# A convolution's rows gathered by head before normalising and transposing, instead of taken in their natural tiles

## The chip, the cores and the metric

The kernel runs on one core of one Trainium2 chip. The metric is the device time of one execution in microseconds (us). A profiled execution gives the trace; its span runs from the first to the last instruction. Engines are TensorE (PE, with PEld for its weight loads), VectorE (DVE), ScalarE (ACT), GpSimd (POOL) and SyncE (SP), which here only issues transfers.

## The reference, cut to what matters

Two layers, each a gated cross attention and a gated feed-forward, on x of shape (8, 256, 512). The change lies in the first layer's "attention", which is a long convolution:

```python
    def _L0_xattn_ref(k, v, q, ssm_kernel, D, head_dim):
        ...
        H = HD // head_dim
        fft_size = 2 * L
        ...
        kv = jnp.einsum('bhil,bhjl->bijhl', k_, v_)
        kv_f = jnp.fft.rfft(kv, n=fft_size)
        kernel_f = jnp.fft.rfft(ssm_kernel, n=fft_size)
        y = jnp.fft.irfft(kv_f * kernel_f, n=fft_size)[..., :L]
        out = y + kv * D[None, None, None, :, None]
        out = jnp.einsum('bijhl,bhil->bjhl', out, q_)
        ...
    x = x + jnp.tanh(g_xattn[0]) * _L0_xattn_ref(ctx_2048, ctx_2048, _layernorm(x, axis=-1), L0_xattn_ssm_kernel, L0_xattn_D, 8)
    x = x + jnp.tanh(g_ffn[0]) * _L0_ffn_ref(_layernorm(x, axis=-1), L0_ffn_w1, L0_ffn_w2, L0_ffn_w3)
    x = x + jnp.tanh(g_xattn[1]) * _L1_xattn_ref(_layernorm(x, axis=-1), ctx_2048, mask_BxS2_bk0)
    x = x + jnp.tanh(g_ffn[1]) * _L1_ffn_ref(_layernorm(x, axis=-1), L1_ffn_w1, L1_ffn_w2, L1_ffn_w3)
```

Context and x have 256 rows per batch, k and v are both the context and q is the normalised x. The 256 rows of a batch are 32 heads of 8 rows; the convolution runs along the 512 columns. Each row is normalised over those 512 columns.

## The kernel before

**Tiles.** x is 2048 rows of 512, kept for the whole kernel in `xs` as 16 natural tiles of 128 rows. A natural tile is half a batch: the even tiles hold heads 0 to 15 of the eight batches, the odd ones heads 16 to 31. The convolution wants positions on the partitions, so every tile is normalised (statistics and their aggregate on DVE, L116 and L117; square root on ACT, L121; reciprocal and the negative mean term on DVE, L126 and L134; the norm itself on ACT, L179, or DVE, L174), turned by four PE transposes into one PSUM tile `tr` (L386), and copied by ACT into the buffer `qT` (`keep_x`, L389; in the opening three of these by DVE, L657). Head 0 needs its 8 rows of every batch, and so all eight even tiles.

**One head.** The convolution is a product with a Toeplitz matrix: `load_toep` (L270) fetches its 128 x 512 strip from `ssm_skip`, a copy of the padded kernel in DRAM to which the skip term D has been added, and `load_ch` fetches the context (L265). ACT doubles the context (`ctx_twice`, cx, L289), POOL multiplies its 36 row pairs (`pair_products`, kv, L302 and L308), PE runs 10 matmuls of 288 columns in two halves (`half_matmuls`, L325), which the profile shows as 6 and 14 instructions, because each fp32 matmul stands there as two (a transpose as one), into one of three PSUM tiles `y`, ACT repeats some columns (`half_wrap`, L335), DVE multiplies by q in three instructions per half (`half_products`, L347, L353, L360), POOL adds the two planes (`add_halves`, L370) and DVE reduces them into `qT` (`reduce_terms`, L375). In steps 12, 14, 19 and 21 (the set `alone`), POOL's sum is left out and DVE reduces both planes (L377). q is doubled before it is used, by one ACT copy per head out of `qT` (`q_twice`, L289).

**Order.** The whole stage is written out by hand: each engine executes its instructions in program order, and a wait holds up all that stands behind it on that engine. After the opening a loop runs over 32 steps h; `half_matmuls(h + 1, 1)` and `half_matmuls(h + 2, 0)` belong to step h. A table of jobs adds other work to the slots of a step ("load", "act", "dve", "pe", "act2", "pool", "late"): the odd x tiles in steps 0 to 12, the absolute values, rounding and clipping of the feed-forward weights (`w0`, `w1`), the transposes back with the first residual (L394, L204, steps 17 to 25), and the statistics for the next stage. All these transfers are issued by SP, also in program order. Strips, contexts and kv have three buffers each, the doubled context and q two.

**The opening** normalises the even tiles in four pairs: two 256 KB tiles per transfer (L259), statistics of the second pair placed before the inverse of the first, `half_matmuls(0, 0)` after the first pair's transposes, the rest of head 0 among those of the other three pairs. Five small transfers go out from ACT's queue (gates, the skip term in two layouts, the padded kernel); the first strip comes directly from the input, and its diagonal gets the skip term from DVE (L286). ACT loads the Tanh table for the gates before the Sqrt table.

Of the kernel before, what the change touches and what calls it, by code (L numbers as in the profile page):

```python
# [9 lines left out]
F32 = mybir.dt.float32  # L10
# [32 lines left out]
def flamingo_gated_kernel(  # L43
# [48 lines left out]
    gates_in = small.tile([P, 4], F32, name="gates_in")  # L92
# [132 lines left out]

    s_conv, s_load, s_y = ExitStack(), ExitStack(), ExitStack()
# [14 lines left out]
    ssm = big.tile([H, P + L], F32, name="ssm")  # L241
    skip = big.tile([H, 1], F32, name="skip")
    d0 = big.tile([P, 1], F32, name="d0")

    anti = wl.tile([P, 3 * L], F32, tag="w0st", name="anti")[:, :P]
# [4 lines left out]
    )  # L250
    ssm_skip = dram.tile([H, P + L], F32, name="ssm_skip")
# [5 lines left out]
    def load_x(ts):  # L257
        sl = slice(ts[0], ts[-1] + 1, 2)
        nc.sync.dma_start(out=xs[:, sl, :], in_=x_tiles[:, sl, :])  # L259
# [3 lines left out]
    def load_ch(h):  # L263
        chs[h] = p3.tile([P, NL * B, HD], F32, tag="ch", name="ch")
        nc.sync.dma_start(out=chs[h].rearrange("p a i -> p (a i)"), in_=ctx_heads[h])  # L265
# [11 lines left out]
    def first_toep():  # L277

        toeps[0] = p3.tile([P, L], F32, tag="toep", name="toep")
        nc.sync.dma_start(  # L280
            out=toeps[0], in_=bass.AP(ssm_pad.tensor, ssm_pad.offset + 1, [[1, P], [1, L]])
        )

    def first_diagonal():
        t = toeps[0][:, :P]
        nc.vector.scalar_tensor_tensor(t, anti, d0[:, 0:1], t, op0=ALU.mult, op1=ALU.add)  # L286

    def twice(out, src):
        nc.scalar.copy(  # L289
            out.rearrange("p a (r i) -> p a r i", r=2),  # L290
            src.unsqueeze(2).to_broadcast([P, NL * B, 2, HD]),
        )

    def ctx_twice(h):
        cxs[h] = p2.tile([P, NL * B, HX], F32, tag="cx", name="cx")
        twice(cxs[h], chs[h])
# [15 lines left out]
    def q_twice(h):  # L312
        qxs[h] = p2.tile([P, NL * B, HX], F32, tag="qx", name="qx")
        twice(qxs[h], qT[:, :, h * HD : (h + 1) * HD])
# [22 lines left out]
    def half_products(h, half):  # L337


        if half == 0:  # L340
            prods[h] = p2.tile([P, 2, NL * B, HD, ND], F32, tag="prod", name="prod")
        prod = prods[h]
        n = 2 * B
        yv = ys.pop((h, half)).rearrange("p k b n -> p (k b) n")
        r = slice(half * n, (half + 1) * n)
        q = qxs[h][:, r, :]
        nc.vector.tensor_tensor(  # L347
            prod[:, 0, r, :, :],
            yv[:, :, W0 : W0 + ND * HD].rearrange("p a (i d) -> p a i d", d=ND),
            view(q, [HX, n], [1, HD], [1, ND]),  # L350
            ALU.mult,
        )
        nc.vector.tensor_tensor(  # L353
            prod[:, 1, r, :, 0].rearrange("p a (r i) -> p a r i", r=2),
            yv[:, :, W0 + ND * HD : W0 + NPAIR].unsqueeze(2).to_broadcast([P, n, 2, ND]),
            view(q[:, :, ND:HX], [HX, n], [ND, 2], [1, ND]),
            ALU.mult,
        )

        nc.vector.tensor_tensor(  # L360
            prod[:, 1, r, :, 1:ND],
            view(yv[:, :, ND - 1 : YB], [YB, n], [ND, HD], [ND - 1, NW]),
            view(q[:, :, HD - NW : HX], [HX, n], [1, HD], [1, NW]),
            ALU.mult,
        )
# [16 lines left out]

    def transpose_x(t, xn):
        tr = trs[t] = ps_tr.tile([P, NL, P], F32, tag="tr", name="tr")
        for c in range(NL):
            nc.tensor.transpose(tr[:, c, :], xn[:, c * P : (c + 1) * P], ident)  # L386

    def keep_x(t):
        nc.scalar.copy(rows[:, :, t * P : (t + 1) * P], trs.pop(t))  # L389
# [132 lines left out]
    lno, lnx, firsts = {}, {}, {}  # L522

    def odd_stats(k):
        mv = small.tile([P, 1, 2], F32, tag="mvo", name="mvo")
        ln_moments(mv, 0, odds[k])
        lno[k] = (mv,)

    def odd_sqrt(k):
        lno[k] += (ln_sqrt(lno[k][0], 1, "o"),)  # L530

    def odd_inverse(k):
        mv, std = lno[k]
        rstd = ln_inverse(std, 1, "o")
        lno[k] = (rstd, ln_nmr(nc.vector, mv, rstd, [0], "o"))

    def odd_norm(k):
        xn = lnx[k] = p2.tile([P, L], F32, tag="xn", name="xn")
        ln_apply_act(xn, odds[k], *lno.pop(k), 0)

    def odd_turn(k):
        transpose_x(odds[k], lnx.pop(k))
# [15 lines left out]
    for k in range(len(odds)):  # L558
        job(k, "load", load_x, [odds[k]])
        job(k + 2, "dve", odd_stats, k)  # L560
        job(k + 2, "late", odd_sqrt, k)
        job(k + 3, "dve", odd_inverse, k)
        job(k + 3, "late", odd_norm, k)
        job(k + 4, "pe", odd_turn, k)
        job(k + 5, "act", keep_x, odds[k])
    for k in range(len(evens)):
        job(17 + k, "pe", back_transpose, evens[k])
        job(18 + k, "dve", back_add, evens[k])
# [10 lines left out]
    steps1 = [2, 7, 8, 9, 10, 12, 13, *range(15, 19), 18, 19, 20, 21, 23]  # L579
# [23 lines left out]


    for g, o in ((g_xattn, 0), (g_ffn, 2)):
        nc.scalar.dma_start(out=gates_in[:, o : o + 2], in_=g.partition_broadcast(P))
    nc.scalar.dma_start(out=d0, in_=ssm_d[0:1].partition_broadcast(P))
    nc.scalar.dma_start(out=ssm, in_=ssm_pad)
    nc.scalar.dma_start(out=skip, in_=ssm_d.rearrange("(h o) -> h o", o=1))
    pairs = [evens[k : k + 2] for k in range(0, len(evens), 2)]  # L610
    load_x(pairs[0])
    load_ch(0)
    first_toep()
    for k in range(1, len(pairs)):
        load_x(pairs[k])
    load_ch(1)
    load_table(AF.Tanh)
    nc.scalar.activation(gates, gates_in, AF.Tanh)
    load_table(AF.Sqrt)

    ps_ = {}

    def pair_stats(k, j):
        if j == 0:
            ps_[k] = (small.tile([P, 2, 2], F32, tag="mvp", name="mvp"),)
        ln_moments(ps_[k][0], j, pairs[k][j])

    def pair_sqrt(k):
        ps_[k] += (ln_sqrt(ps_[k][0], 2, "p"),)

    def pair_inverse(k, by_act):

        mv, std = ps_[k]
        rstd = ln_inverse(std, 2, "p")
        nmr = ln_nmr(nc.vector, mv, rstd, by_act, "p")
        both = wl.tile([P, 3 * L], F32, tag="w0st", name="xnp")
        xn = [both[:, :L], both[:, L : 2 * L]]
        for j in range(2):
            if j not in by_act:
                ln_apply(xn[j], pairs[k][j], mv, rstd, j)  # L640
        ps_[k] = (xn, rstd, nmr)

    def pair_norm(k, by_act):
        xn, rstd, nmr = ps_[k]
        for j in by_act:
            ln_apply_act(xn[j], pairs[k][j], rstd, nmr, j)

    def pair_turn(k, js=(0, 1)):
        for j in js:
            transpose_x(pairs[k][j], ps_[k][0][j])  # L650

    def pair_keep(k, j, eng):
        t = pairs[k][j]
        if eng is nc.scalar:
            keep_x(t)
        else:
            nc.vector.tensor_copy(rows[:, :, t * P : (t + 1) * P], trs.pop(t))  # L657

    pair_stats(0, 0)
    pair_stats(0, 1)  # L660
    ctx_twice(0)
    pair_products(0)
    pair_sqrt(0)
    pair_stats(1, 0)
    pair_inverse(0, (0, 1))
    pair_norm(0, (0, 1))
    first_diagonal()
    pair_stats(1, 1)
    pair_turn(0)
    pair_sqrt(1)  # L670
    half_matmuls(0, 0)
    nc.vector.tensor_add(ssm[:, P : P + 1], ssm[:, P : P + 1], skip)
    nc.sync.dma_start(out=ssm_skip, in_=ssm)
    load_toep(1)
    load_ch(2)
    load_toep(2)
    load_ch(3)
    pair_stats(2, 0)
    pair_keep(0, 0, nc.scalar)
    pair_inverse(1, (0,))  # L680
    pair_norm(1, (0,))
    pair_keep(0, 1, nc.scalar)
    pair_stats(2, 1)
    pair_turn(1, (1, 0))
    pair_sqrt(2)
    pair_stats(3, 0)
    half_matmuls(0, 1, (0,))
    pair_keep(1, 1, nc.scalar)
    pair_inverse(2, (0,))
    pair_norm(2, (0,))  # L690
    pair_stats(3, 1)
    pair_turn(2, (1, 0))
    pair_sqrt(3)
    pair_keep(1, 0, nc.scalar)
    pair_inverse(3, (0,))
    pair_norm(3, (0,))
    ctx_twice(1)
    pair_products(1)
    pair_keep(2, 1, nc.vector)
    half_wrap(0, 0)  # L700
    pair_turn(3, (1, 0))
    pair_keep(2, 0, nc.vector)
    pair_keep(3, 1, nc.scalar)
    pair_keep(3, 0, nc.vector)
    half_matmuls(0, 1, (1,))
    q_twice(0)
    half_wrap(0, 1)
    ctx_twice(2)
    pair_products(2)
    half_matmuls(1, 0)  # L710
    half_products(0, 0)
# [3 lines left out]
    for h in range(H):  # L715
# [5 lines left out]
        if h + 1 < H:  # L721
            q_twice(h + 1)
# [4 lines left out]
        if h > 0 and h - 1 not in alone:  # L727
            reduce_terms(h - 1, True)
        if h in alone:
            reduce_terms(h, False)  # L730
        else:
            add_halves(h)
        if h + 1 < H:
# [588 lines left out]
```

## Time and profile before

| | |
|---|---|
| three executions | 767.15, 771.16 and 1251.91 us, median 771.16 |
| the profiled execution | 769.82 us, its span 768.0 us |
| mean granted TensorE clock | 0.993 |
| busy: PE, DVE, ACT, POOL | 728.3, 594.1, 366.5, 254.3 us |
| first convolution matmul | 14.28 us from the span's start |
| last convolution matmul begins | 190.9 us |
| 640 convolution matmul instructions | 164.2 us of PE, 413 ns mean of one |
| 62 wrap copies of 192 columns, ACT | 303 ns each |
| 64 copies of 512 columns (cx and qx), ACT | 619 to 621 ns each |
| statistics of one tile, DVE | 684 and 182 ns |
| transfers of ch, toep and one x tile | 4.1, 3.8 and 4.7 us from issue to landing, medians |

The slices of the profile are fortieths of the span, each digit the busy share in tenths. In a table of stretches, each engine has its busy time and the number of its instructions. In a timeline a line gives start, duration, engine, source line, operation, result and source, and in brackets the idle time of the engine before it with what ended that. Matmuls overlap, so that a matmul's duration is longer than its distance from the next. A line of the waits names the waiting group, the group it waited for, the total in us, how often, and the longest.

### The profile page before, as it was taken

The numbers are of one execution on the slowest core, as the hardware profiler recorded it, in microseconds if no ns is written. First come the engines' busy times: TensorE is split into PE (matmuls) and PEld (weight loads), VectorE is DVE, ScalarE is ACT, GpSimd is POOL, SyncE is SP. The second block draws the span as 40 slices with busy tenths as digits, with TensorE's granted clock in tenths as the row PEclk, the third lists the DMA queues.
The fourth block names the chain that finished last, engine by engine and source line by source line (L and its number), as shares of the span: only waits on it lengthen the run. The fifth ranks groups of instructions, "written<-read, shape, count | busy, mean of one in ns | idle before, by whom it ended". The sixth has DMA issues, their size and how long they took to land.

```text
span 768.0 us, 10145 instructions
## 1 busy us (share of the span) xinstructions
PE 728.3 (95%) x3247; PEld 535.5 (70%) x3260; DVE 594.1 (77%) x1188; ACT 366.5 (48%) x670; POOL 254.3 (33%) x356
## 2 busy tenths in 40 slices
PE   3999999898899999898989999999999999999997
PEld 2777777676454444465656888888888888888885
DVE  4699879898978888686796977777887777787664
ACT  4477876665677876557742222222222322222221
POOL 1788987888774534434111200000000000000000
PEclk9999999999999999999999999999999999999999
DMA  6675676631236667575612434333543343344433
GB/s 186 194 246 167 198 233 213 244 83 28 34 80 141 151 134 185 149 248 155 197 40 52 89 83 89 79 82 77 90 83 84 77 83 90 70 96 84 85 84 82
DMA packets 130166, 93.39 MB, mean 122 GB/s; under 512 B 70656, under 2 KB 108032, under 8 KB 130112
## 3 DMA queue, kind: packets, MB, share of 16 engines
q1 hardware_dynamic: 129328, 92.38, 46.9%
q0 software_dynamic: 256, 0.26, 0.4%
q8 instruction: 26, 0.43, 0.2%
q14 instruction: 28, 0.23, 0.1%
q10 hardware_dynamic: 528, 0.08, 0.1%
HBM read 71.91 MB, written 4.54 MB: 100 GB/s over the span
## 4 chain that ended last, share of the span: by engine, by line
PE 54%; DVE 9%; POOL 3%; DMA 3%; issue 3%; ACT 3%; SPq 0%; another core or an unknown queue 0%; DVEq 0%; ACTq 0%; POOLq 0%
PE pa L1069 15%; PE pb L1069 15%; PE po L1211 14%; PE po L808 2%; PE pb L791 2%; PE pa L791 2%; DMA hqT<-qh 2%; PE po L903 2%; DVE st L116 1%; DVE am L482 1%; PE ps L874 1%; DVE hh L800 1%; DVE xs L204 1%; PE tr L1058 1%; DMA w1st<-in_L_w2t 1%
## 5 line engine op out<-in xcount | busy, mean ns | idle before, releaser
L325 PE MATMUL y<-kv,toep 128*128 128x288 f32 x640 | 164.2, 413 | 5.0 <-DVE prod L360 4.7
L325 PEld LDWEIGHTS y<-kv,toep 128*128 128x128 f32 x640 | 121.1, 193 | 39.2 <-issue 4.3
L1078 DVE SCALAR_TENSOR_TENSOR hh<-pb,wmean,sl 128x512 f32<-128x512 f32 x64 | 47.8, 747 | 75.2 <-PE pb L1069 47.1
L1069 PE MATMUL pa<-w,hi 128*128 128x512 f32 x256 | 103.6, 405 | 0.7 <-ACT hi L1050 0.7
L1211 PE MATMUL po<-w,hi 128*128 128x512 f32 x256 | 101.3, 396 | 0.6 <-ACT hi L1050 0.6
L1069 PE MATMUL pa<-w,lo 128*128 128x512 f32 x256 | 100.4, 392 | 0.8 <-DVE lo L1052 0.8
L1211 PE MATMUL po<-w,lo 128*128 128x512 f32 x256 | 100.1, 391 | 0.2 <-DVE lo L1052 0.2
L1069 PE MATMUL pb<-w,lo 128*128 128x512 f32 x256 | 99.8, 390 | 0.0
L1069 PE MATMUL pb<-w,hi 128*128 128x512 f32 x256 | 99.7, 389 | 0.0
L1077 ACT ACTIVATE sl<-pa,wmean 128x512 f32<-128x512 f32 x64 | 44.1, 688 | 109.2 <-PE pa L1069 109.2
L1050 ACT CAST hi<-v 128x512 fp32r<-128x512 f32 x64 | 39.3, 619 | 103.5 <-DVE v L1204 99.9
L302 POOL TENSOR_TENSOR kv<-cx 128x1024 f32<-128x1024 f32 x32 | 60.6, 1893 | 37.5 <-ACT cx L289 37.5
L370 POOL TENSOR_TENSOR prod<-prod 128x1024 f32<-128x1024 f32 x28 | 66.2, 2363 | 2.6 <-DVE prod L360 2.6
L791 PEld LDWEIGHTS <-xqT 128*128 128x128 bf16 x384 | 37.5, 98 | 41.4 <-issue 4.5
L1069 PEld LDWEIGHTS pa<-w,hi 128*128 128x128 f32 x256 | 48.1, 188 | 14.6 <-ACT hi L1050 0.9
L1069 PEld LDWEIGHTS pa<-w,lo 128*128 128x128 f32 x256 | 48.2, 188 | 11.0 <-DVE lo L1052 1.2
L1211 PEld LDWEIGHTS po<-w,hi 128*128 128x128 f32 x256 | 48.1, 188 | 10.8 <-ACT hi L1050 1.0
L1211 PEld LDWEIGHTS po<-w,lo 128*128 128x128 f32 x256 | 48.1, 188 | 10.6 <-DVE lo L1052 0.9
L1069 PEld LDWEIGHTS pb<-w,hi 128*128 128x128 f32 x256 | 48.0, 188 | 10.2
L1069 PEld LDWEIGHTS pb<-w,lo 128*128 128x128 f32 x256 | 48.1, 188 | 10.1
L1052 DVE TENSOR_TENSOR lo<-v,hi 128x512 fp32r<-128x512 f32 x64 | 44.0, 690 | 13.6 <-ACT hi L1050 12.1
L347 DVE TENSOR_TENSOR prod<-y,qx 128x512 f32<-128x512 f32 x64 | 43.6, 681 | 12.8 <-ACT y L335 8.9
(132 smaller groups left out, 1316.0 us busy)
## 6 DMA issues: line engine op xcount, KB each, us to landing
sT<-d SPq DMA_DIRECT2D x64, 256.0 KB, 4.2
toep<-ssm_skip SPq DMA_DIRECT2D x31, 256.0 KB, 3.8
ch<-in_ctx_heads SPq DMA_DIRECT2D x32, 128.0 KB, 4.1
w1a<-in_L_w1t SPq DMA_DIRECT2D x8, 512.0 KB, 4.5
w1a<-in_L_w2t SPq DMA_DIRECT2D x8, 512.0 KB, 4.2
w1st<-in_L_w1t SPq DMA_DIRECT2D x16, 256.0 KB, 3.5
w1st<-in_L_w2t SPq DMA_DIRECT2D x16, 256.0 KB, 3.9
cT<-in_ctx_t SPq DMA_DIRECT2D x8, 512.0 KB, 4.4
```

The lines of the kernel that those rows point to most:

```text
L302: nc.gpsimd.tensor_tensor(kv[:, :, 0 : ND * HD].rearrange("p a (i d) -> p a i d", d=ND), cx[:, :, 0:HD].unsqueeze(3).to_broadcast([P, NL * ...
L325: nc.tensor.matmul(y[:, k, :, W0 : W0 + NPAIR], toeps[h][:, d * P : (d + 1) * P], kvs[h][:, mi * B : (mi + 1) * B, :].rearrange("p b n -> ...
L347: nc.vector.tensor_tensor(prod[:, 0, r, :, :], yv[:, :, W0 : W0 + ND * HD].rearrange("p a (i d) -> p a i d", d=ND), view(q, [HX, n], [1, H ...
L370: nc.gpsimd.tensor_tensor(flat[0], flat[0], flat[1], ALU.add)
L791: nc.tensor.matmul(pp[:, :fw], xqT[:, c, :], w0q[i][:, c, f0 : f0 + fw], start=(c == 0), stop=(c == NL - 1),)
L808: nc.tensor.matmul(po, hqT[:, c, :], w0q[2][:, c, :], start=(c == 0), stop=(c == NF0 - 1))
L1050: nc.scalar.copy(hi, v)
L1052: nc.vector.tensor_tensor(lo, v, hi.bitcast(F32), ALU.subtract)
L1069: nc.tensor.matmul(pp, xT[k][:, c, :], w1q[i][:, c, f0 : f0 + 512], start=(c == 0 and k == 0), stop=(c == NL - 1 and k == 1),)
L1077: nc.scalar.activation(sl, pa, AF.Silu, scale=wmean1[:, 0:1])
L1078: nc.vector.scalar_tensor_tensor(hh, pb, wmean1[:, 1:2], sl, op0=ALU.mult, op1=ALU.mult)
L1211: nc.tensor.matmul(po, hT[b][k][:, c, :], w1q[2][:, b * NL + c, :], start=(b == 0 and c == 0 and k == 0), stop=(b == NB - 1 and c == NL - ...
```

## The change

A gathered tile j holds the 16 rows of heads 2j and 2j + 1 of all eight batches, 128 rows in all. One such tile is loaded, normalised, transposed and doubled for two heads, in every second step. The natural tiles are still needed for the residual, so they are loaded as well: the even ones in steps 1 to 15, the odd ones in steps 14 to 28; until then their places in `xs` hold the gathered tiles. `q_twice` copies 128 x 1024 out of the PSUM tile for two heads, and `qT` receives only results. The opening takes tiles 0, 1 and 2; it runs 13 small matmuls beforehand, spreads the gates and the skip term over the partitions with a small matmul instead of broadcasting transfers, and takes the first two strips directly from the input. The context has two buffers instead of three. In the loop `reduce_terms(h - 1, True)` stands behind `add_halves(h)` or `reduce_terms(h, False)` instead of before it. The table for Tanh is loaded in step 0 and the one for Sqrt again in step 1. The steps of the `w1` sums are others. An unused tile of 24 columns takes the place of one that is gone.

```diff
+    const.tile([P, 24], F32, name="apart")
...
-    def load_x(ts):
-        sl = slice(ts[0], ts[-1] + 1, 2)
-        nc.sync.dma_start(out=xs[:, sl, :], in_=x_tiles[:, sl, :])
+    def load_x(t):
+        nc.sync.dma_start(out=xs[:, t, :], in_=x_tiles[:, t, :])
+    def place(j):
+        return odds[j % len(odds)]
+    def load_gathered(j):
+        nc.sync.dma_start(
+            out=xs[:, place(j), :],
+            in_=bass.AP(x.tensor, x.offset + j * HX * L, [[S * L, B], [L, HX], [1, L]]),
+        )
...
-        chs[h] = p3.tile([P, NL * B, HD], F32, tag="ch", name="ch")
+        chs[h] = p2.tile([P, NL * B, HD], F32, tag="ch", name="ch")
...
-    def q_twice(h):
-        qxs[h] = p2.tile([P, NL * B, HX], F32, tag="qx", name="qx")
-        twice(qxs[h], qT[:, :, h * HD : (h + 1) * HD])
+    def q_twice(j):
+        qx = p2.tile([P, NL * B, 2, HX], F32, tag="qx", name="qx")
+        tr = trs.pop(("q", j)).rearrange("p c (b h i) -> p (c b h) i", h=2, i=HD)
+        nc.scalar.copy(
+            qx.rearrange("p a h (r i) -> p (a h) r i", r=2),
+            tr.unsqueeze(2).to_broadcast([P, NL * B * 2, 2, HD]),
+        )
+        for k in range(2):
+            qxs[2 * j + k] = qx[:, :, k, :]
...
-    for k in range(len(odds)):
-        job(k, "load", load_x, [odds[k]])
-        job(k + 2, "dve", odd_stats, k)
-        job(k + 2, "late", odd_sqrt, k)
-        job(k + 3, "dve", odd_inverse, k)
-        job(k + 3, "late", odd_norm, k)
-        job(k + 4, "pe", odd_turn, k)
-        job(k + 5, "act", keep_x, odds[k])
+    LATE = [2, 4, 6, 8, 10, 11, 15, 16]
+    for j in range(1, H // 2):
+        if j >= 3:
+            job(2 * j - 6 if j < 8 else max(j - 8, 2 * j - 18), "load", load_gathered, j)
+        if 3 <= j < 8:
+            job(2 * j - 5, "dve", g_stats, j)
+            job(2 * j - 5, "late", g_sqrt, j)
+        elif j >= 8:
+            h = LATE[j - 8]
+            job(h, "dve", g_stats, j)
+            if j % 2:
+                job(h, "late", g_sqrt, j - 1)
+                job(h + 1, "dve", g_inverse, j - 1)
+        if 2 <= j:
+            if j < 8:
+                job(2 * j - 4, "dve", g_inverse, j)
+            job(2 * j - 4, "late", g_norm, j)
+        job(2 * j - 2, "pe", g_turn, j)
+    job(0, "act", tanh_gates)
+    job(1, "act", load_table, AF.Sqrt)
     for k in range(len(evens)):
+        job(2 * k + 1, "load", load_x, evens[k])
+        job(14 + 2 * k, "load", load_x, odds[k])
...
-    steps1 = [2, 7, 8, 9, 10, 12, 13, *range(15, 19), 18, 19, 20, 21, 23]
+    steps1 = [2, 4, 6, 7, 8, 8, 9, 10, 10, 12, 16, 18, 18, 20, 24, 26]
...
     nc.scalar.dma_start(out=ssm, in_=ssm_pad)
-    nc.scalar.dma_start(out=skip, in_=ssm_d.rearrange("(h o) -> h o", o=1))
...
+    for v, o in ((ssm_d, 4), (g_xattn, 0), (g_ffn, 2)):
+        n = v.shape[0]
+        nc.scalar.dma_start(out=singles[:, o : o + n], in_=v.rearrange("(o n) -> o n", o=1))
+    load_gathered(0)
     load_ch(0)
+    direct_toep(0)
+    load_gathered(1)
     load_ch(1)
+    direct_toep(1)
+    load_gathered(2)
+    load_ch(2)
     load_table(AF.Sqrt)
+    pt = ps_tr.tile([P, 512], F32, tag="tr", name="warm")
+    for _ in range(13):
+        nc.tensor.matmul(pt[:, :P], ident, ident, start=True, stop=True)
+    g_stats(0)
+    ctx_twice(0)
+    pair_products(0)
+    g_sqrt(0)
+    g_inverse(0)
+    g_norm(0)
+    g_stats(1)
+    g_turn(0)
+    wide = ps_tr.tile([P, 512], F32, tag="tr", name="wide")
+    nc.tensor.matmul(wide[:, : 4 + H], ones[0:1, :], singles, start=True, stop=True)
...
+    nc.vector.tensor_copy(wide_sb, wide[:, : 4 + H])
+    diagonal(0)
+    nc.vector.tensor_add(ssm[:, P : P + 1], ssm[:, P : P + 1], wide[:H, 64:65])
     nc.sync.dma_start(out=ssm_skip, in_=ssm)
     load_toep(2)
     load_ch(3)
+    diagonal(1)
+    half_matmuls(0, 0)
+    q_twice(0)
+    ctx_twice(1)
+    pair_products(1)
+    g_sqrt(1)
+    g_stats(2)
+    g_inverse(1)
+    half_wrap(0, 0)
+    half_matmuls(0, 1)
+    g_norm(1)
+    g_sqrt(2)
     ctx_twice(2)
     pair_products(2)
+    half_products(0, 0)
+    half_wrap(0, 1)
     half_matmuls(1, 0)
     half_wrap(1, 0)
...
-        if h + 1 < H:
-            q_twice(h + 1)
+        if h % 2 and h + 1 < H:
+            q_twice((h + 1) // 2)
...
         half_products(h, 1)
-        if h > 0 and h - 1 not in alone:
-            reduce_terms(h - 1, True)
         if h in alone:
             reduce_terms(h, False)
         else:
             add_halves(h)
+        if h > 0 and h - 1 not in alone:
+            reduce_terms(h - 1, True)
```

`g_stats`, `g_sqrt`, `g_inverse`, `g_norm` and `g_turn` do for a gathered tile what the `odd_` functions did for an odd one; from tile 8 on square root and inverse serve two tiles at once. `direct_toep` and `diagonal` are the old first strip and its diagonal with the head as an argument.

## The prediction

> **What bounds the kernel now.** I read the page's slices first, then busy time by stretches, then the timeline of the opening, the waits, and the timeline around the one large hole.
>
> ```profile
> PE   3999999898899999898989999999999999999997
> DVE  4699879898978888686796977777887777787664
> POOL 1788987888774534434111200000000000000000
> ```
>
> TensorE is full nearly everywhere (728.3 of 768.0 us). Slice 1 is the exception. So the change can win what PE idles in the opening, plus holes in the convolution, and little else.
>
> ```profile
> core 0: us, PE busy (x) PEld busy (x) DVE busy (x) ACT busy (x) POOL busy (x), PEclk, DMA share, GB/s
> 0.00:14.28 14.28, 1.74 (x9) 1.77 (x9) 5.40 (x18) 6.20 (x12) 3.60 (x12) 1.00 0.65 195
> 14.28:24.24 9.96, 9.58 (x46) 7.39 (x45) 6.21 (x17) 6.05 (x12) 2.31 (x2) 1.00 0.24 79
> 24.24:43.64 19.40, 19.40 (x82) 15.20 (x80) 15.36 (x30) 9.72 (x22) 17.38 (x12) 1.00 0.90 276
> 138.75:148.02 9.27, 7.21 (x26) 5.25 (x24) 8.61 (x15) 5.55 (x9) 9.27 (x8) 0.82 0.67 245
> 148.02:191.16 43.14, 41.57 (x177) 31.50 (x175) 38.68 (x86) 25.66 (x48) 35.36 (x26) 1.00 0.25 69
> ```
>
> Row 1 is the time before head 0's first matmul. Row 2 is head 0 with 24 transposes among its 20 matmul instructions. Row 3 is heads 1 to 4 at PE's pace: 19.40/4 = 4.85 us. Row 4 is head 23, row 5 heads 24 to 31 (5.39 each).
>
> ```profile
> 10.34 0.69 DVE L116 BATCH_NORM_STATS2 st<-xs 128x6 f32<-128x512 f32 x1 [2.94 <-DMA xs<-in_x]
> 11.59 1.52 ACT L179 ACTIVATE xnp<-xs,nmr,rstd 128x512 f32<-128x512 f32 x2 [3.23 <-DVE nmr L134]
> 12.54 1.94 PE L386 MATMUL tr<-ident,xnp 128*128 128x128 f32 x8 [12.54 <-ACT xnp L179]
> 14.28 3.09 PE L325 MATMUL y<-kv,toep 128*128 128x288 f32 x6
> 24.43 0.32 SPq L270 DMA_DIRECT2D toep<-ssm_skip  x1
> ...
> 43.83 0.33 SPq L270 DMA_DIRECT2D toep<-ssm_skip  x1
> 48.68 0.33 SPq L270 DMA_DIRECT2D toep<-ssm_skip  x1
> 53.97 0.33 SPq L270 DMA_DIRECT2D toep<-ssm_skip  x1
> ```
>
> DVE sits 2.94 us until the second x pair lands, with the first pair's inverse queued behind it; ACT, PE and head 0 follow. A toep load is issued when a head's last matmul frees its buffer, so these lines mark heads: 4.85 us without transposes, 5.29 with one tile's four (0.44).
>
> ```profile
> DVE qT L375 <- POOL prod L370: 9.2, 13, 1.7
> PE y L325 <- DVE prod L360: 4.7, 6, 2.1
> ```
> ```profile
> 132.66 0.62 ACT L289 COPY cx<-ch 128x512 f32<-128x512 f32 x1 [2.03 <-DMA ch<-in_ctx_heads]
> 133.36 1.89 POOL L302 TENSOR_TENSOR kv<-cx 128x1024 f32<-128x1024 f32 x1 [3.10 <-ACT cx L289]
> ...
> 138.02 1.22 DVE L375 TENSOR_REDUCE qT<-prod 128x256 f32<-128x1024 f32 x1 [1.74 <-POOL prod L370]
> 139.16 2.28 DVE L377 TENSOR_REDUCE qT<-prod 128x256 f32<-128x2048 f32 x1
> ...
> 142.86 6.78 PE L325 MATMUL y<-kv,toep 128*128 128x288 f32 x20 [2.06 <-DVE prod L360]
> ```
>
> That is head 23: a context load 2.03 us late, POOL late by 3.10, DVE held 1.74 by POOL's sum with the long reduction of head 21 behind it, PE idle 2.06, then 20 matmuls in 6.78 us instead of 4.85 at a granted clock of 0.82. It lost 9.27 - 5.29 = 4.0 us. From 24.24 to 191.16 the ideal is 31 x 4.85 + 16 x 0.44 = 157.4 of 166.9 us: 9.5 us are holes.
>
> **Part A, the opening.** Head 0 needs one gathered tile instead of eight. One 256 KB x tile goes first where 512 KB landed at 5.68; I take 4.5 (4.0 to 5.7). Context 0, landed at 6.07, has 256 KB less ahead, at 173 KB/us over the first 10 us 1.4 us: 4.7, with a doubled table load gone from ACT's front (1.28 + 0.20); cx at 5.0 to 5.6. Square root 0.29, inverse to norm 0.42, norm 0.81: xn at 7.2; four transposes at the rate of the first eight (1.94/2 = 0.97): 8.2; two small matmuls 0.3. kv: 5.65 + 1.89 + 0.45 = 8.0, not last. DVE is last: statistics of tile 1 stand before the diagonal, and x1 is the same 896th KB that landed at 8.16 (toep 0): 0.8 to 9.0, copy 0.3, diagonal 0.34, so head 0 starts at 9.7 (8.5 to 12), not 14.28. POOL's second kv starts after context 1 is doubled, behind the 1.1 us q copy: ready near 12.5, before PE asks. So head 0's 20 matmuls run without transposes, in 4.85 at the open clock, or spaced 0.48 as the first six here (3.09 us) while it is half.
>
> Which clock, the warm-up decides. Its 13 fp32 matmuls are 26 instructions of 128 columns; at the 0.24 us of the first eight transposes they last 6.3 us, from 1.6 (the identity is made at 1.4) to 7.9, and less once the clock opens (the third eight took 1.04). They keep PE from nothing but the first transposes, by 0.7 at most, which the wait for x1 hides. But from there to 9.7 PE has six small instructions, and head 23 shows that a hole of 2.06 was followed by the half clock and cost 6.78 - 4.85 = 1.9. I take half of that, 0.9 (0 to 3.4, fourteen matmuls at 0.24 more). Head 1 starts at 9.7 + 4.85 + 0.9 = 15.45, not 24.24: **-8.8** (-10.4 to -5.5).
>
> The Trainium skill, TensorE: Matmul & The Clock Gate, Part 1, states that about 3.4 us of sustained work opens the clock and an idle window of that length, free-running, closes it. By this the warm-up is long enough and the gap after it just short enough, so the 0.9 would be 0 and the sum 0.9 us better; the hole of 2.06 before head 23 was shorter than the page's window, and the row decides.
>
> **Part B, transposes moved.** The tiles leave the opening for steps 0 to 28. Heads 1 to 31 carry 15 tiles instead of 8: 7 x 0.44 = **+3.1**. Three fall into heads 26, 28 and 30, where DVE sets the pace (row 5: 5.39 against 4.85), so 1.3 of it is hidden: **+1.8**.
>
> **Part C, ACT.** 16 copies of 1024 from PSUM replace 32 q copies of 0.62 and 16 of 0.58. No such row; scaling the 0.30 (192 columns) and 0.62 (512) rows gives 1.12 (bounds 0.62 and 2 x 0.62): 17.9 against 29.1 us. ACT is 9.72 of 19.40 busy, so the 11 us saved are worth 0. The Tanh load and the return to Sqrt (2 x 1.48) go to steps 0 and 1, with the wrap copies behind them; ACT's idle half covers it; without cover 3.0 us.
>
> **Part D, the reduction's order.** In steps 12, 14, 19 and 21 the long reduction, which waits for nothing on POOL, now precedes the one that waits. In step 21 it fills the 1.74 us; the hole of 2.06 shrinks below one us and the slow clock after it should go: -3.3 of the 4.0 (-4.0 to 0). Step 12 has the same wait with 1.08 us, head 14 lost 1.4: -1.0 (-1.4 to 0). **-4.3.**
>
> **Part E, what gets tighter.** DVE: thirteen tiles' statistics and inverses in the loop instead of eight. Starts of neighbours lie 3.75 us apart per head (2 x (0.60 + 0.22 + 0.46) + 1.2), so two heads with two statistics (0.82 each) and 0.3 to 0.75 of inverses take 9.45 to 9.9 of the 10.14 us of PE: 93 to 98%, where it was 92%. DMA: every x tile comes twice, 4.2 MB more; SP issues 16 more transfers at 0.42, which its waits cover. Steps 0 to 3 ask for 7,168 KB instead of 5,888 (three x tiles and one w1 piece more) in 4 x 4.85 + 2 x 0.44 = 20.3 us; row 3 moved 276 GB/s at a share of 0.90, so about 300 KB/us: 23.9 us, a backlog of 3.6 us that drains later (some 250 KB/us asked). toep has a spare head; ch, now with two buffers, waits on SP for kv two heads back, with the x and weight loads queued behind it. **+2.1** (0 to +10).
>
> Sum: -8.8 + 1.8 - 4.3 + 2.1 = -9.2. The profiled execution took 769.82 us around its span of 768.0 (1.3 below the median of 771.16): **760.6**. After 191.16 nothing is changed but addresses, worth 0.
>
> **Rivals.** (1) *All holes close.* Clock open at once, DVE in step: -9.7 + 1.8 - 7.5 = -15.4, 754. For it: 5.4 of the 9.5 us lie at heads 14 and 23, where DVE stood behind POOL. Against: part E. (2) *Given back.* PE's lead vanishes because DVE sets the pace in steps 1 to 10 (98% in odd pairs) or the first loads wait for others as L259 did for 2.2 us: 3 to 7 us lost, 764 to 767. (3) *Slower: the two context buffers.* ch(h+4) is issued when kv(h+2) is done, lands, is doubled (0.62) and multiplied (2.35): latency + 0.4 + 0.6 + 2.35 per two heads, 10.14 us of PE. It decides from a latency of 6.8 us. In 24.24 to 43.64 ch took 4.3 us, x 5.1, w0st 6.3, and the backlog adds up to 3.6. At 9 us each of the first eight pairs loses 2.2: +17.6, 778. Against: the backlog lasts some four steps, which alone costs 2 to 4 us. (4) *It does not do what it says*: POOL, 17.38 of 19.40 busy, not x, limits heads 1 to 5, so an earlier start only waits: 767 to 770.
>
> **How the numbers follow.** Forecast 0.50 (757 to 764), (1) 0.22, (2) and (4) 0.19, (3) 0.09. Bound to 8 in 10: 752 to 773, which takes the earliest start with all holes closed and half of (3). Over 2%, about what a measurement of this kernel can tell from no change, faster means below 755.7: all of (1) but its edge and a little of the forecast, 0.24; slower means above 786.6, the far end of (3), 0.05; within 0.71.
>
> **What would show it.** Head 0's first matmul near 9.7 and head 1 near 15.5; the last convolution matmul near 182; 16 ACT copies of 1024 at about 1.1; no hole over 1 us around head 23. Wrong if DVE waits for x1 past 9 us, if the first 20 matmuls lie 0.48 apart, or if ACT waits for ch in steps 1 to 8.

## The result, and the profile after

The changed kernel takes 771.52 us (median of 20 runs, 767.75 to 776.92); the kernel before took 767.27 in 20 runs beside it, of which one slow run of 1251.91 us is left out of the ratio. The ratio is 1.0059 with a 95% interval of 1.0045 to 1.0074: a little slower, inside the 2% that counts as no change and inside the range, but on the other side of no change from the 760.6 forecast. The profiled execution took 775.78 us, its span 774.0, so it lies 4.3 above the median; the shown one of before, 769.82, lies 2.6 above its own.

Stretches of the changed kernel; the columns are those of the table in the prediction. The rows are the time before head 0, head 0, heads 1 to 4 and the start of head 5, and the rest of head 5 with heads 6 to 8:

```profile
core 0: us, PE busy (x) PEld busy (x) DVE busy (x) ACT busy (x) POOL busy (x), PEclk, DMA share, GB/s
0.00:10.51 10.51, 7.01 (x35) 6.50 (x35) 2.62 (x9) 4.69 (x8) 3.61 (x12) 1.00 0.60 163
10.51:17.12 6.61, 6.61 (x20) 4.93 (x21) 4.47 (x8) 1.97 (x6) 3.97 (x3) 0.74 0.29 83
17.12:38.26 21.14, 21.14 (x93) 16.70 (x92) 16.30 (x35) 13.82 (x27) 16.37 (x12) 1.00 0.90 261
38.26:60.00 21.74, 19.15 (x77) 14.30 (x76) 16.37 (x39) 11.73 (x24) 14.43 (x12) 0.92 0.82 238
```

Head 0 starts at 10.51 instead of 14.28 and takes 6.61 us at a granted clock of 0.74; head 1 starts at 17.12 instead of 24.24, 7.1 us earlier. Heads 1 to 4 run at PE's pace. In the fourth row PE idles 2.6 us and the clock is down. Head 8 starts at 56.97, only 2.1 us earlier than before (59.07): most of the lead is gone by then.

The difference of the two profiled executions, 775.78 - 769.82 = +6.0, splits in three. Until head 1: -7.1. From there to the start of the last convolution matmul (190.16; before 190.86) it was 166.63 us and is 173.04: +6.4. From that matmul to the end of the span it was 577.2 and is 583.9: +6.7.

The timeline of the changed kernel's opening:

```profile
8.95 0.69 DVE L117 BATCH_NORM_STATS2 st<-xs 128x6 f32<-128x512 f32 x1 [1.51 <-DMA xs<-in_x]
9.03 1.01 ACT L329 COPY qx<-tr 128x1024 f32<-128x1024 f32 x1 [0.75 <-PE tr L566]
10.05 0.35 DVE L302 SCALAR_TENSOR_TENSOR toep<-opening,toep 128x128 f32<-128x128 f32 x1
10.64 2.04 DVE L302 SCALAR_TENSOR_TENSOR toep<-opening,toep 128x128 f32<-128x128 f32 x1 [0.18 <-DMA toep<-in_ssm_pad]
10.64 1.89 POOL L315 TENSOR_TENSOR kv<-cx 128x1024 f32<-128x1024 f32 x1 [1.69 <-ACT cx L306]
```

DVE waits for x1 until 8.95, and the diagonal that head 0 needs (10.05) stands behind its statistics. The copy of 1024 takes 1.01 us. The second diagonal, the same instruction as the first, takes 2.04 us instead of 0.35, beside POOL's kv.

The timeline of the changed kernel around heads 5 and 6, the strip and the context that they wait for, first their issues, then who waited:

```profile
32.56 0.33 SPq L283 DMA_DIRECT2D toep<-ssm_skip  x1
34.33 0.33 SPq L278 DMA_DIRECT2D ch<-in_ctx_heads  x1
...
45.00 3.22 PE L345 MATMUL y<-kv,toep 128*128 128x288 f32 x6 [2.59 <-DMA toep<-ssm_skip]
45.30 0.62 ACT L306 COPY cx<-ch 128x512 f32<-128x512 f32 x1 [5.60 <-DMA ch<-in_ctx_heads]
45.99 1.89 POOL L315 TENSOR_TENSOR kv<-cx 128x1024 f32<-128x1024 f32 x1 [4.96 <-ACT cx L306]
```

The strip issued at 32.56 landed at 44.87, 12.3 us later (in the kernel before the strips of this stretch took 3.8 to 5.1), and PE, ACT and POOL all stood for it or for the context beside it. This is the largest hole in the loop.

The timeline of the changed kernel around head 23, where the large hole was:

```profile
136.67 2.29 DVE L397 TENSOR_REDUCE qT<-prod 128x256 f32<-128x2048 f32 x1
136.99 5.02 PE L345 MATMUL y<-kv,toep 128*128 128x288 f32 x20
138.87 1.21 DVE L395 TENSOR_REDUCE qT<-prod 128x256 f32<-128x1024 f32 x1
142.28 0.89 PE L345 MATMUL y<-kv,toep 128*128 128x288 f32 x3
```

The long reduction comes first, DVE waits for nobody, and from head 22's second half PE goes on without the hole of 2.06 us and at full clock: head 23 takes 5.29 us, where it took 9.27.

### The profile page after: what moved, and what is told of

Same layout as the page of the kernel before. It is cut to its first block, busy times and chain, and to the rows that moved or that the text cites. A ratio compares the mean times of both kernels' runs of the same rounds, so it can differ in the third digit from the quotient of the medians.

```text
span 774.0 us, 10198 instructions
## 1 busy us (share of the span) xinstructions
PE 739.1 (95%) x3277; PEld 542.5 (70%) x3290; DVE 594.0 (77%) x1187; ACT 361.5 (47%) x646; POOL 254.0 (33%) x356
## 4 chain that ended last, share of the span: by engine, by line
PE 60%; DVE 11%; POOL 6%; issue 4%; ACT 3%; DMA 2%; another core or an unknown queue 0%; SPq 0%; DVEq 0%; ACTq 0%; POOLq 0%
PE pa L1056 15%; PE pb L1056 15%; PE po L1198 14%; PE po L795 3%; PE pb L778 3%; PE pa L778 3%; PE y L345 2%; PE po L890 2%; DMA hqT<-qh 2%; POOL kv L315 1%; POOL prod L390 1%; DVE st L117 1%; PE ps L861 1%; DVE am L494 1%; DVE qT L395 1%
```

## The experiments

Theory: the loads are late, because the gathered tiles are read with the 8 batches as slowest dimension and only 8 of the 16 engines carry such a load, and because the early steps ask for more. Rivals: the bytes alone; the reductions' order; the opening alone; and, for what follows the convolution, chance. Each run stood beside runs of the kernel before on the same chip; their medians were 767.26 to 767.73. Ratios compare all runs of both sides, not the medians, so the two can differ by some tenths of a per cent.

**The kernel before, profiled again.**

> The kernel before, unchanged, to see how far its own trace varies. In the two traces at hand the convolution of the changed kernel ends 0.7 us earlier (last matmul at 190.16 against 190.87), and yet its span is 6.0 us longer; from the convolution's end on it had five stretches of half clock against two. Theory: the stretches behind the convolution come and go from run to run in both kernels, each worth 1.3 to 1.7 us, so a second trace of the kernel before has its convolution's end within 2 us of 190.9 but another number of half-clock stretches behind it, and its runs of 765 to 771 us follow their mean clock. Rival: the code behind the convolution is really slower in the changed kernel, and then the stretches here are the same two, at the same places.

767.08 us, ratio 0.9997 (0.9987 to 1.0007). In this trace head 23 took 7.04 us, without the half clock that made it 9.27 in the one shown before the prediction, and the last convolution matmul began at 188.25 instead of 190.86. So 2.2 us of the hole that the change was to close were the shown execution's own. Behind the convolution it has one window of half clock where the shown one has two.

**Rows outermost, q doubled in two copies.** 

```diff
-            in_=bass.AP(x.tensor, x.offset + j * HX * L, [[S * L, B], [L, HX], [1, L]]),
+            in_=bass.AP(x.tensor, x.offset + j * HX * L, [[L, HX], [S * L, B], [1, L]]),
...
-        nc.scalar.copy(
-            qx.rearrange("p a h (r i) -> p (a h) r i", r=2),
...
         for k in range(2):
+            nc.scalar.copy(
+                view(qx[:, :, k, :], [2 * HX * B, NL], [2 * HX, B], [HD, 2], [1, HD]),
...
```

> The gathered tile is loaded row first (16 rows outside, 8 batches inside) instead of batch first, so that the transfer's slowest dimension is 16 instead of 8; q is doubled in two copies of 512 instead of one of 1024. Theory (ring imbalance): the gathered loads run on 8 of 16 DMA engines (their semaphore jumps by 8 at once and climbs by 8 at landing), so engines 0 to 7 are the bound in steps 0 to 8, latencies there are 7 to 12 us, and the 6 us of holes at heads 5 to 9 come from that: latencies fall to 4 to 7 us, the holes at heads 5, 6 and 9 go, the time falls by 4 to 6 us to about 766. Rival (bytes): 7.2 MB in four steps is too much however it is spread: latencies stay above 8 us, the time within 1 us of 771.5. Third (context buffers): latencies fall, but ACT still waits for ch at heads 5 and 6.

766.27 us, ratio 1.0007 (0.9982 to 1.0031): 5.2 below the changed kernel. x0 landed at 4.59 instead of 5.73. The profiled execution was the slowest of its ten (773.14): its first diagonal fell beside POOL's kv, took 2.04 us, and head 0 began only at 12.01, at half clock.

**Natural even tiles loaded later**, in steps 10 to 17 instead of 1 to 15.

> The natural even tiles are loaded in steps 10 to 17 instead of 1, 3, ... 15: four 256 KB loads fewer in steps 1 to 7, all of them on 16 engines, the gathered ones stay on 8. Bytes theory: 1.0 of about 8.9 MB less in the crowded steps, the backlog at head 5 shrinks by two tiles (1.7 us at 300 KB/us) and the 3.0 us hole falls to 1 us or less: 768 to 769. Ring theory: engines 0 to 7 lose only half of these bytes, the hole falls by 0.8 us, and the time by about 1 us: 770.5.

769.65 us, ratio 1.0045 (1.0026 to 1.0064): 1.9 lower than the changed kernel, whose interval overlaps with this one. The hole behind head 5 stayed, 2.63 us (2.59 in the changed kernel), with a strip of 12.4 us behind it: fewer bytes alone don't mend it.

**The old order of the reductions in the changed kernel.**

> The changed kernel with the loop's reduction where it was before, ahead of the long one in steps 12, 14, 19 and 21. Theory (the forecast's part D): the hole at head 23 comes back, 2 us and perhaps the half clock after it, so 2 to 4 us slower, about 774. Rival: the hole at head 23 came from a late context load behind the old w1 loads (2.03 us late), and the new steps of w1 have taken it away, not the order: within 1 us of 771.5, and no hole over 1 us at head 23.

773.82 us, ratio 1.0094 (1.0068 to 1.0120): 2.3 worse by four runs, which lie inside the range of the changed kernel's twenty, and not where it was expected. Head 23 took 5.29 all the same, as the rival had it; holes of 1.48 and 2.31 us stood at heads 13 and 14, then a half clock: head 14 took 9.60.

**The new order alone in the kernel before.**

> The kernel before with only the loop's reduction moved behind the long one (part D of the forecast alone). Forecast: the hole of 2.35 us at head 23 and that of 1.4 at head 14 shrink below 1 us: 2 to 4 us faster, 763 to 765. Rival: the holes sit on POOL's sum and context loads, the reduction that moved back is needed by no one sooner, but head 14's hole stays (it stayed at 1.4 to 1.5 us in the changed kernel): 1 to 2 us faster, all of it from head 23.

765.97 us, ratio 0.9984 (0.9961 to 1.0006). Head 14 went from 6.22 to 5.19 us, head 23 to 5.66. The order is worth some 1.8 us by the medians, though the interval just holds no change.

**Eight groups in the kernel before, twice.** First the eight odd x loads of the loop were written as 8 groups of 16 neighbouring rows.

> The kernel before, with the same eight odd x tiles to the same places at the same steps 0 to 7, but each read as 8 groups of 16 rows, so that only the shape of the transfer is the gathered one's and 8 of 16 engines carry it. Ring theory: in steps 0 to 3, 24 to 44 us, engines 0 to 7 get (5888 - 1024)/2 + 1024 = 3456 KB at 150 KB/us = 23 us where 19.4 pass, latencies of the loads there rise from 4.3 to 6.4 us to 7 us and more, the first holes appear at heads 4 to 8, and the time rises by 1 to 4 us to 768.5 to 771. Rival (it is the bytes, or the waits of the new step order, that hurt): the same as before within 0.7 us, latencies unchanged.

767.55 us, ratio 0.9999 (0.9979 to 1.0018), latencies as before. It tested nothing: the semaphores of these loads still climbed by 16 single steps, as if the neighbouring rows had been merged into one dimension of 128. So the groups were spread, with other rows of x in these tiles:

```diff
-        nc.sync.dma_start(out=xs[:, sl, :], in_=x_tiles[:, sl, :])
+        rows8 = bass.AP(x.tensor, x.offset + ts[0] * HX * L, [[S * L, 8], [L, 16], [1, L]])
...
+            in_=x_tiles[:, sl, :] if len(ts) > 1 else rows8,
```

> The kernel before, with its eight odd x loads of the loop read as 8 groups of 16 rows that lie 256 rows apart, so that the groups can't be merged; they hold other rows and the output is not the reference's; the work is the same. In the run with 8 groups of neighbouring rows the semaphores climbed by 16, so the groups had been merged and that run tested nothing. Theory 1 (eight engines): these loads now raise their semaphore by 8 at once; each takes 1 to 3 us longer to land and so do the toep and ch loads beside it; with one a step and little else asked for, the median rises by 0 to 3 us. Theory 2 (bytes): 0, latencies as before.

767.55 us, ratio 1.0001 (0.9986 to 1.0016). Now each of these semaphores made one jump about 1 us after the issue and then eight steps at the landing, and no byte more was asked for, yet the strips and contexts issued from 29.7 to 45 us took 5.6 to 8.2 us instead of 4.0 to 4.5 in the run with neighbouring rows (4.0 to 5.1 in the kernel before). The strips issued from 29 to 45 us, with their number, size and median time in us from issue to landing, in the kernel before and then in this run:

```profile
toep<-ssm_skip SPq DMA_DIRECT2D x4, 256.0 KB, 4.5
```
```profile
toep<-ssm_skip SPq DMA_DIRECT2D x4, 256.0 KB, 6.7
```

The mechanism is there; the kernel before, with three contexts and one x tile a step, still hides 8 us. Its time did not move.

**Only the reading order changed in the changed kernel.** 

> The changed kernel, with the gathered loads alone read with the 16 rows of a batch outermost instead of the 8 batches; q is doubled as before in one copy of 1024, so the transposed columns hold the rows of q in another order and the output is not the reference's; the work is the same. Theory 1 (eight engines): a 256 KB load whose slowest dimension is 8 lands late because 8 of 16 engines carry it; then x0 lands near 4.6 instead of 5.73, latencies in steps 1 to 8 fall, the hole at head 5 shrinks below 1.5 and the median is 765 to 768. Theory 2 (bytes): only the amount asked for in steps 0 to 8 counts; x0 may land earlier, but the median stays 770 to 773. Theory 3 (the two copies): what the row-first version won came from two copies of 512 in place of one of 1024; then 770 to 773 too, with x0 at 4.6 and the q copies still 1.00.

768.83 us, ratio 1.0009 (0.9988 to 1.0031): 2.7 below the changed kernel, one above the band of theory 1 and below that of both others. In head 5, which took 5.27 us instead of 7.60, PE had no idle gap over 0.1 us. The ten microseconds in which the strip for head 6 was under way, as stretches of the changed kernel and then of this one:

```profile
25.00:35.00 10.00, 10.00 (x45) 7.86 (x45) 8.07 (x18) 6.51 (x14) 8.80 (x6) 1.00 1.03 330
35.00:45.00 10.00, 7.41 (x31) 5.51 (x30) 9.14 (x20) 3.55 (x7) 5.02 (x4) 0.98 0.91 244
```
```profile
25.00:35.00 10.00, 10.00 (x45) 7.90 (x44) 7.72 (x15) 5.70 (x12) 7.46 (x5) 1.00 1.02 328
35.00:45.00 10.00, 9.95 (x43) 7.30 (x43) 8.24 (x20) 5.63 (x11) 7.93 (x6) 1.00 1.04 335
```

From 35 to 45 us the changed kernel moved 244 GB/s while its transfers took 9 to 12 us; with the rows outermost, and nothing else changed, it moved 335, and PE was busy 9.95 instead of 7.41 us. The ten microseconds before do not differ (330 and 328). The other three runs with rows outermost moved 333, 322 and 358 from 35 to 45 us, the one with the late tiles alone 233. In the profiled execution this opening lost a race:

```profile
8.43 0.69 DVE L117 BATCH_NORM_STATS2 st<-xs 128x6 f32<-128x512 f32 x1 [2.12 <-DMA xs<-in_x]
9.53 2.04 DVE L302 SCALAR_TENSOR_TENSOR toep<-opening,toep 128x128 f32<-128x128 f32 x1
9.54 1.89 POOL L315 TENSOR_TENSOR kv<-cx 128x1024 f32<-128x1024 f32 x1 [1.72 <-ACT cx L306]
11.68 8.55 PE L345 MATMUL y<-kv,toep 128*128 128x288 f32 x23 [3.32 <-POOL kv L315]
```

This is the timeline of its opening. x0 came at 4.60, so POOL's second kv came earlier too, but DVE still waited for x1, and the first diagonal now began together with kv: 2.04 us instead of 0.35, and head 0 at 11.68. Whether that is why the median is not lower was not shown: it is one trace. The run with two copies of q stands alike by its ratio, 1.0007 against 1.0009.

**One warm-up matmul instead of thirteen.**

> The changed kernel with one warm-up matmul instead of thirteen. My theory: the clock closes in the gap before head 0 whether or not the warm-up ran (head 0 lasted 6.61 us with it), so the opening keeps its 10.5 and 17.1 within 1 us and the median stays within 2 us of 771.5. Rival: the warm-up opens the clock for the four transposes and the small matmuls, or shortens head 0's slow stretch; without it head 0 lasts 9.6 (20 matmuls at 0.48), head 1 starts 2 to 3 us later, and the median is 773 to 775. Second rival: the transposes come 0.5 to 0.9 earlier because PE is free when xn is ready, head 0 starts below 10.0 and the median is 770 to 771.

770.51 us, ratio 1.0048 (1.0026 to 1.0070): 1.0 lower, which is within my 2 us, but head 0 began at 11.26, took 7.68 us and head 1 came at 18.94, 1.8 later than with the warm-up. So the warm-up does shorten the opening, as the first rival had it, and the end does not feel it: head 6 began at 45.39 against 45.00.

**The statistics of tile 1 behind the first diagonal.**

```diff
-    g_stats(1)
     g_turn(0)
...
     load_ch(3)
+    g_stats(1)
     diagonal(1)
```

> The changed kernel with the statistics of tile 1 moved on DVE behind the first diagonal and the skip sum, so that head 0 no longer stands behind the load of x1; gathered loads, natural loads and q copies are as in the changed kernel. Theory (two separate losses): the opening's part comes back, head 0 at 9.3 to 9.8 and at the open clock, head 1 at 14.2 to 15.2 (17.12 in the changed kernel), while the hole at head 5 of 1.5 to 3 us with the loads of 10 to 12 us stays: the median is 768 to 770. Rival 1 (one loss): the loop is late by its bytes whatever the start, so a start 2 to 3 us earlier only waits at heads 5 to 9, whose holes grow by as much: 770.5 to 772.5. Rival 2 (the opening was all of it): below 767.

771.61 us, ratio 1.0059 (1.0036 to 1.0083): nothing won. Rival 1 holds: head 1 began at 16.50, 0.6 earlier (not the 2 to 3 expected), and the hole behind head 5 grew by 0.6, from 2.59 to 3.19. Head 6 began at 44.97, as in the changed kernel (45.00) and the one with late tiles (44.94): the strip decides, not the start.

**Rows outermost and late tiles; then the statistics behind the diagonal as well.**

> The changed kernel with the gathered loads on 16 engines and the natural even tiles loaded in steps 10 to 17. Latencies in steps 0 to 8 of the 16-engine version were still 8 to 10 us (bytes), so both causes add up: no hole over 0.5 us at heads 5 to 9, where that version lost 2.2 us: 764 to 765. If the bytes are hidden anyway: 766.3, as without.

> As the run before it, and in the opening the statistics of tile 1 stand behind the first diagonal and the skip sum instead of ahead of them. Theory: in the 16-engine version the first diagonal took 2.04 us instead of 0.35 because POOL's second kv ran beside it (both DVE operands lie in SBUF), and head 0 began at 12.0 instead of 10.2; with the statistics behind, the diagonal runs at about 8.7, while POOL is idle, and no longer waits for x1: head 0 begins at 8.9 to 9.2, head 1 near 14 to 15.5, the spread of the runs falls (no runs at 772), 761.5 to 763.5. Rival: the first matmuls then run at half clock for longer, since PE's warm-up lies further from them in neither case, and the start is worth only half: 763.5 to 765.

The two together: 765.06 us, ratio 0.9970 (0.9950 to 0.9990). All three: **762.44 us**, ratio 0.9940 (0.9921 to 0.9959), 9.1 below the changed kernel. By their intervals both versions lie below both kernels, against the kernel before by less than 2%. In the two traces head 1 starts at 14.65 and 13.87, head 6 at 39.96 and 40.38, the last convolution matmul at 183.02 and 182.38. The opening of the last, as a timeline:

```profile
8.49 0.35 DVE L302 SCALAR_TENSOR_TENSOR toep<-opening,toep 128x128 f32<-128x128 f32 x1
8.83 0.68 DVE L117 BATCH_NORM_STATS2 st<-xs 128x6 f32<-128x512 f32 x1
8.95 7.27 PE L345 MATMUL y<-kv,toep 128*128 128x288 f32 x29 [0.80 <-issue]
9.43 1.90 POOL L315 TENSOR_TENSOR kv<-cx 128x1024 f32<-128x1024 f32 x1 [1.71 <-ACT cx L306]
```

The diagonal is done before kv begins, head 0 starts at 8.95 and takes 4.93 us: at an open clock, as the forecast had wanted it. The statistics, worth nothing alone, are worth 2.6 by the medians here, where the loads no longer take it back; the two intervals just overlap. The trace of the two changes together is the fastest of its ten runs (761.48): there the first diagonal began 0.10 us before kv and still took 0.35. With the statistics behind it, it begins 0.94 before kv. That the median gains because no run loses this race any more fits the narrower spread (761.21 to 764.97 against 761.48 to 767.92), but with one trace of each it is not shown.

## Why the prediction was wrong, point by point

The profiled execution came 15.2 us above the forecast, 775.78 against 760.6: A missed by 1.7, B by 1.3, D by 0.3, E by 5.2 and the part behind the convolution by 6.7. The median lies 4.3 lower than this execution; if that is all windows of half clock behind the convolution, which is an estimate, E is the largest miss in most executions.

**A, the opening: right in kind, -7.1 instead of -8.8.** Head 0 was foreseen at 9.7 and came at 10.51, because x0 landed at 5.73, the far end of the bounds, and x1 at 8.93 instead of the 8.16 that it took from toep 0. With rows outermost x0 landed at 4.40 to 4.60, the 4.5 of the forecast. The clock cost 1.8 (6.61 - 4.85), not 0.9, and the count of windows below says why: the window from 7.20 to 10.60 held only 1.36 us of PE's work. Where head 0 began at 8.95 and 9.73 the clock stayed open; of the kernels with the warm-up, the six that began at 10.17 or later had one or two windows at half clock. In the step "which clock, the warm-up decides" the row of head 23 pointed the right way and the gap "just short enough" did not save the clock. The Trainium skill, TensorE: Matmul & The Clock Gate, Part 1, is right here about the window, 3.41 us long and free-running, but calls the one that closes the clock idle; this one was not.

**B, the moved transposes: about +3.1, not +1.8.** Before, heads 24, 25 and 26 lasted 5.29, 5.29 and 5.43 us without a tile; now heads 24 and 26, with one, last 5.73 and head 25, without one, 5.29. Heads 26, 28 and 30, where the forecast hid 1.3, grew by 0.30, 0.44 and 0.43: under DVE's pace a tile still cost nearly its 0.44.

**C, ACT: right.** The copies take 0.99 to 1.01 us (1.12 estimated). That the difference is worth nothing fits the two runs with rows outermost, 1.0007 with two copies and 1.0009 with one.

**D, the reductions' order: the hole at head 23 went, but not by the order alone; wrong at head 14, and too large for most executions.** Head 23's hole is gone, -4.0 in the profiled execution. With the old order in the changed kernel it was gone too (5.29 us), so something else in the change closes it as well, and which part no run shows; in the kernel before the order alone closed most of it (5.66 instead of 7.04). Head 14 loses 1.45 us as before (6.74 instead of 5.29 with its tile; before, 6.22 instead of 4.85): from 86.47 to 93.44 DVE has hardly a gap, since the statistics of a gathered tile, the long reduction of 2.29 us, one of 1.21 and the tile's inverse now follow each other there. And a sum made on one execution took over its accident: 2.2 of the 4.0 were this execution's own, above all a half clock that another execution of the same kernel did not have (its hole was 1.51 us instead of 2.06): the window that ended at 144.0 held 1.36 us of PE's work, while the least of any window around head 23 in the other execution, where the windows fell otherwise, was 1.90. The order alone gave 1.8 by the medians in the kernel before, in an interval that just holds no change, not 4.3.

**E is the step that failed.** It took +2.1 with "a backlog of 3.6 us that drains later", at 300 KB/us, and "toep has a spare head". The loop lost 6.4; with B at 3.1 and D at -4.0, E was 7.3 us, inside its bounds of 0 to +10. Of these 4.4 lie at heads 5 and 6; in the version of 762.44 the same sum leaves 2.8 (its loop lost 1.9), so by this estimate some 4.5 were the loads, and the rest has no run of its own. The rate was the error: it came from a stretch of the kernel before in which every load ran on all engines. The new loads run on 8, and the changed kernel moved 244 GB/s where the same requests with rows outermost moved 335. The semaphore of the late strip shows the halves: seven of its sixteen steps came 4.9 to 5.6 us after the issue and one at 7.7, the other eight at 11.3 to 12.3; with rows outermost the strip issued at 34.52 had fifteen within 8.5 us and the last at 10.2. SP, whose waits were to cover the 16 more issues, waited itself for transfers to land. A strip that takes 12.3 us is later than a spare head can cover, so heads 5 and 6 lost 2.75 and 1.61 us. The Trainium skill, DMA: Bandwidth & Descriptors, "Why a DMA increments its semaphore by 16 and not by 1", says that a transfer from these queues is spread over the largest number up to 16 that divides the slowest dimension of both sides, and that the engines not used are counted off at once. The one jump and the eight steps agree. The diff shows the 8 batches (`B`) as the slowest dimension, and I read over it.

**"After 191.16 nothing is changed but addresses, worth 0" failed** by 6.7 us in the profiled execution. The work there is the same, but not the clock. From the start of the last convolution matmul to the end of the span it took, by the number of half-clock windows in that part, in fourteen traces:

```
1 window   576.4  576.5  576.7  576.8  577.1  577.3  577.7  578.1
2 windows  577.2  577.4  579.5  579.6
4 windows  581.6
5 windows  583.9  (the changed kernel)
```

So it is about 575 us, and some 1.7 for each window of 3.41 us at half clock. When such a window comes can be counted. Three windows of the changed kernel that ended where the clock went down, as stretches:

```profile
7.20:10.60 3.40, 1.36 (x10) 0.97 (x10) 1.57 (x6) 2.38 (x4) 1.75 (x2) 0.99 0.71 188
41.30:44.70 3.40, 1.11 (x5) 0.55 (x3) 3.23 (x7) 0.00 (x0) 0.00 (x0) 1.00 0.70 252
321.20:324.60 3.40, 1.05 (x7) 0.81 (x8) 1.12 (x3) 2.97 (x7) 2.57 (x12) 1.00 0.56 105
```

PE was busy 1.36, 1.11 and 1.05 us of 3.40. The third row is a hole of 2.7 us behind the convolution that before does not have; another of 3.2 ends at 308, where before has one of 2.9 that ends at 315. The clock changes only on a grid of 3.41 us (every recorded stretch of one clock is a multiple of it, but for the one that a trace cuts off at its end), so whether a hole of 2 to 3 us costs a window depends on how it lies on the grid, and the grid lies otherwise in every execution. Over all runs the mean granted clock of the changed kernel was 0.989 (median of 20), of before 0.997; a window is 0.0022 of it (half of 3.41 us, of 774), so there are some 3.6 windows more, in the profiled execution one at head 0 and one at head 6. The one at head 0 does not compare: the clock records of the kernel before begin only at 17.70 us, so its slow first matmuls (six in 3.09 us) count as full clock in its mean and in its row from 14.28. As an estimate, of the 4.3 us between the medians 1.9 come from the end of the convolution (190.16 against 188.25 in the second trace of before) and the rest from windows behind it. Why its later holes are 3.2 and 2.7 us, and 2.4 and 2.3 in the fastest version, was not settled.

**The rivals.** "Given back" (2) named the first loads and the loss of 3 to 7 us, and comes nearest; its 764 to 767 lacked the windows. "Two context buffers" (3) had the right symptom, ACT waiting 5.60 for a context, and the latency it asked for (10.9 us, above 6.8), but not the cause: with the two buffers kept, other loads and the opening's new order gave 762.44. A third buffer was not tried. Of the signs of being wrong that the prediction named, this wait was the one that came. "All holes close" (1) and POOL as the limit (4) did not happen: POOL itself waited 4.96 us.

## What to carry to other kernels

Look at the slowest dimension of every new access pattern, on both sides, before taking a transfer's price from a row: a load of the same bytes on half the engines is slower itself and slows those beside it. Here an opening that started earlier was worth nothing until the loads of the steps behind it landed earlier too; look for the first wait on a transfer after it, and ask what time that has by itself. And check on a second execution whether a hole that is to be closed has its size in both.

## What the runs showed of the hardware

- The first 256 KB load landed at 5.63 to 5.98 us in the five traces of the changed kernel and its variants with 8 as its slowest dimension, and at 4.40 to 4.60 in the four with 16. From 35 to 45 us the queue moved 233 to 290 GB/s in the five and 322 to 358 in the four (the kernel before, which asked for less, 289).
- From 28.5 to 47.6 us seven or eight transfers were always under way in the changed kernel (two to six in the kernel before): eight semaphores serve in turn, and the next issue waits for the eighth before it (the late strip was issued at 32.56, when the eighth before it had landed at 32.49, the context behind it at 34.33, after a landing at 34.25). So one slow load also delays the issue of those behind it.
- The diagonal, one DVE instruction with two operands in SBUF, took 0.35 us alone, and also where it began 0.10 us before POOL's multiplication. It took 1.56 to 2.04 in the six cases where it began together with that multiplication, of 1.89 to 2.00, or behind it; each time it ended 0.15 us after POOL's. That can set the start of the whole kernel.
- PE need not be idle for its clock to fall. Of the full-clock windows of the 3.41 us grid in the fourteen traces, up to the last matmuls, all 29 in which matmuls ran for 1.42 us or less were followed by a window at half clock; of the six between 1.43 and 1.56 three were; above that only two were, both in an opening (1.83 and 2.06).
